# A recommendation kernel on Trainium2: the attention's weighing and sum moved to VectorE with tokens on partitions

## The chip, the cores and the metric

The kernel runs on one core of one Trainium2 chip. The metric is the device time of one execution in microseconds (us). The engines of the core are TensorE (PE in the profile; PEld is its weight load), VectorE (DVE), ScalarE (ACT), GpSimd (POOL) and SyncE (SP). SBUF is the working memory with 128 partitions; PSUM takes TensorE's products and can be read and written by VectorE and ScalarE.

## The reference

For 4096 users, each with a history of 200 items, the kernel computes a small attention over the history and then a three-layer head. All numbers are float32; an embedding has D = 64 elements.

```
u = u_emb[user]; it = i_emb[item]; c = c_emb[cate]; h = i_emb[hist]      # h: 200 x 4096 x 64
feat = concat([h, it, h - it, h * it])                                   # 256 wide
a = dice(feat @ au_W1 + au_b1, au_alpha, axis=1)                         # 36 wide, moments over the users
w = a @ au_W2 + au_b2                                                    # one weight per user and history line
cur = sum over the 200 lines of w * h
z = concat([u, it, c, cur])
z = dice(z @ W1 + b1, ...); z = dice(z @ W2 + b2, ...); out = z @ W3 + b3
dice(x, alpha) = x * (p + alpha * (1 - p)),  p = sigmoid((x - mean) / sqrt(var + 1e-8))
```

The moments of the attention's dice are taken over all 4096 users of one history line, so a line's gate can only be computed when all tiles of that line have passed the first layer.

## The kernel before, in words

A history line is cut into eight tiles of 512 users (ND = 8). One *step* k handles one tile; there are 200 x 8 = 1600 steps. Line and column of a step are `l, c = divmod(k, ND)`.

**Gathers.** `fetch(k)` issues the tile's rows: 16 indirect DMAs of 128 rows each on GpSimd's queue (line L119 of the profile), into `rows[k % 4]`, with tokens (users) on partitions and 16 x 64 elements along them. Each takes its 128 row numbers from one column of `idx`, which SyncE loads a line ahead. In every second line one of the 16 is left to SyncE: for column c = 7 (`SIDES`) SyncE reads 128 addresses into registers and issues 128 single-row DMAs into `side` (`rows_by_sync`, spread over the steps by `ask`); ScalarE copies that side into `rows` (L301). So a step has 16 gathers, or 15 in one of 16 steps.

**First layer.** `turn(k-1)`: four VectorE transposes (L150) turn the rows, in blocks of 32 x 32, into `hT`, with the features on partitions and two users' groups side by side; TensorE multiplies `hT` by `blk_h` into the PSUM tile `px`; ScalarE copies `hT` to the PSUM tile `ph` (L304). `product(k-1)`: VectorE multiplies `ph` by the item's features `itT` into `hm` (L307), and TensorE adds `hm` times `blk_m` to `px`. `hidden(k-2)`, one step later: VectorE adds the item's own part `itp` to `px`, giving x in `xs` (L292), and `measure` takes its statistics (L297). After the eighth tile `moments` turns the statistics into a scale and a shift (small operations, L313 to L327, and L164 to L166).

**Second layer,** nine steps behind the gather (`LAG = 9`): `gate` has ScalarE compute the dice's gate into the PSUM tile `pg` (L280, L281), `weights` multiplies it by x into `y` in SBUF (L284), and TensorE multiplies `y` by `blk_w`, blocks of ones, into `wb`: the sum over the 36 hidden values appears as w on all the partitions of a user's group. `weigh` then has VectorE compute (wb + b2) * hT in place (L288) and add it to `curT[c]` (L289).

**Order.** Everything is issued in the order of the program (a manual schedule); each engine works through its own list, with semaphores between engines. The order within a step is that of `step`:

```python
fetch(k); hidden(k - 2); measure(k - 2); moments after the eighth tile; gate(k - 9)
turn(k - 1); weights(k - 9); product(k - 1); weigh(k - 9)
```

The 200 lines are run as a hardware loop of three passes of 54 lines (`LPB = 54`) and 38 lines written out behind it; at each pass's end all engines meet at a barrier. Ahead of the loop stand the item's gathers (8 tiles, with transposes and `itp`) and the loading of the weights. In the written-out tail the last steps are interleaved with the head's gathers of categories and users (16 tiles); then follow the head's layers, with moments over all users between them.

Buffers: `rows` 4, `hT` 9 (kept until `weigh`), `xs` 8, `curT` 8, each 128 x 1024 float32.

Of the kernel before, what the change touches and what calls it, by code (L numbers as in the profile page):

```python
# [9 lines left out]
I32 = mybir.dt.int32  # L10
# [10 lines left out]
LPB = 54  # L21
ROWS = 4
LAG = 9
XR = 8
IDX = 3
SIDES = (7,)
EVERY = 2
PART = 8
# [5 lines left out]
def din_kernel(  # L34
# [67 lines left out]
    hT = [make(f"hT{i}", P, CD) for i in range(LAG)]  # L102
    xs = [make(f"xs{i}", P, CD) for i in range(XR)]
    itT = [make(f"itT{c}", P, CD) for c in range(ND)]
    curT = [make(f"curT{c}", P, CD) for c in range(ND)]
    hm = make("hm", P, CD)
    y = make("y", P, CD)
# [23 lines left out]
    def load_hist_ids(i, l, whole):  # L131
# [3 lines left out]
        if whole:  # L135
            nc.sync.dma_start(idx[i][:, NC:], r_hist[ds(l, 1), NC * P :].rearrange("l p -> p l"))

    def load_addresses(m, l):
        nc.sync.dma_start(addr[m % 3], r_hist[ds(l, 1), NC * P :])

    def scale_addresses(m):
        nc.vector.tensor_scalar_mul(addr[m % 3], addr[m % 3], ROW)
# [27 lines left out]
    blk_i = make("blk_i", P, P)  # L170
    blk_m = make("blk_m", P, P)
    blk_w = make("blk_w", P, P)
    au_w = make("au_w", P, 4, A)
# [7 lines left out]
    def attention_weights():  # L181
        nc.vector.memset(eps, EPS)
        for t in (blk_h, blk_i, blk_m, blk_w, au_bias, au_al, au_w2):
            nc.vector.memset(t, 0.0)
        nc.sync.dma_start(au_bias2, au_b2.partition_broadcast(P))
        for e in range(2):
            w = au_W1.rearrange("(g d) a -> d g a", d=D)[e * S : (e + 1) * S]
            for g in range(2):
                r = quarter(e, g)
                nc.sync.dma_start(au_w[r], w)  # L190
                for q, (a0, n) in enumerate(halves):
                    c, a = quarter(q, g, n), slice(a0, a0 + n)
                    nc.vector.tensor_add(blk_h[r, c], au_w[r, 0, a], au_w[r, 2, a])
                    nc.vector.tensor_sub(blk_i[r, c], au_w[r, 1, a], au_w[r, 2, a])
                    nc.vector.tensor_copy(blk_m[r, c], au_w[r, 3, a])
                    nc.vector.memset(blk_w[r, quarter(q, g)], 1.0)
# [25 lines left out]
    lanes, lane = (y[:, ts(i, P)].bitcast(I32) for i in range(2))  # L222
# [34 lines left out]
    def rows_by_sync(m, part):  # L257
        p0 = part * PART
        _, at = nc.values_load_multi_w_load_instructions(
            addr[m % 3][:, p0 : p0 + PART],  # L260
            engines=(mybir.EngineType.SP,), min_val=0, max_val=ROW * (V - 1),
            skip_runtime_bounds_check_because="the DMA checks the address against the table",
        )
        for j, a in enumerate(at):
            row = flat[ds(a, ROW)].rearrange("(o d) -> o d", o=1)
            nc.sync.dma_start(side[m % 3].bitcast(U8)[p0 + j : p0 + j + 1], row)

    def has_side(k):
        l, c = divmod(k, ND)
        return c in SIDES and l % EVERY == EVERY - 1  # L270
# [12 lines left out]
    def weights(k):  # L283
        nc.vector.tensor_mul(y, pg, xs[k % XR])  # L284
        layer(wb, [(blk_w, y)])

    def weigh(k):
        nc.vector.scalar_tensor_tensor(wb, wb, au_bias2, hT[k % LAG], ALU.add, ALU.mult)  # L288
        nc.vector.tensor_add(curT[k % ND], wb, curT[k % ND])  # L289

    def hidden(k):
        nc.vector.tensor_add(xs[k % XR], px, itp[k % ND])  # L292
# [6 lines left out]
    def turn(k):  # L299
        if has_side(k):  # L300
            nc.scalar.copy(rows[k % ROWS][:, TD - 1], side[k // ND // EVERY % 3])  # L301
        transpose(hT[k % LAG], rows[k % ROWS])
        layer(px, [(blk_h, hT[k % LAG])], last=False)
        nc.scalar.copy(ph, hT[k % LAG])  # L304

    def product(k):
        nc.vector.tensor_mul(hm, ph, itT[k % ND])  # L307
        layer(px, [(blk_m, hm)], first=False)
# [44 lines left out]
    def ask(k, end):  # L353
        m, part = divmod(k + 1, EVERY * ND)
        if m * EVERY + EVERY - 1 < end:
            rows_by_sync(m, part)

    def steps(l0, n, more):
        for k in range(n * ND):
            l, c = divmod(k, ND)  # L360
            far = l + EVERY
            if c == 0 and l + 1 < n + more:
                load_hist_ids((l + 1) % IDX, l0 + l + 1, l % EVERY == EVERY - 1)
            if l % EVERY == EVERY - 1 and far < n + more * EVERY:
                if c == 2:
                    load_addresses(far // EVERY, l0 + far)
                if c == 4:
                    scale_addresses(far // EVERY)
            ask(k, n + more * EVERY)
            step(k)  # L370

    with tc.manual_schedule():
        load_ids(ids[0], r_item)
        load_hist_ids(0, 0, True)
        load_addresses(0, EVERY - 1)
# [6 lines left out]
        for t in curT:  # L382
            nc.vector.memset(t, 0.0)
# [6 lines left out]
        scale_addresses(0)  # L390

        for c in range(ND + 1):
            if c < ND:
                for n in range(TD):
                    j = column(c, n)
                    gather(rows[c % ROWS], ids[0][:, j : j + 1], n, i_emb)
            if c:
                transpose(itT[c - 1], rows[(c - 1) % ROWS])
                layer(px, [(blk_i, itT[c - 1])])
                nc.scalar.activation(itp[c - 1], px, AF.Identity, bias=au_bias)  # L400
        layer(px, [(blk_m, hm)])
        nc.vector.memset(rows[-1 % ROWS], 0.0)
        ask(-1, L)
        head_weights()

# [6 lines left out]
    za = [hT[(K - LAG + c) % LAG] for c in range(ND)]  # L412
    zb = [xs[(K - XR + j) % XR] for j in range(2)]
# [6 lines left out]
    def head_fetch(k, j):  # L420
        c, u = divmod(j, 2)
        for n in range(TD):
            i = column(c, n)
            gather(rows[k % ROWS], ids[1 + u][:, i : i + 1], n, (c_emb, u_emb)[u])

    def head_layer(j):
        c, u = divmod(j, 2)
        if u == 0:
            pairs = ((2, ucT[j % 4]), (1, itT[c]), (3, curT[c]))
        else:  # L430
            pairs = ((0, ucT[j % 4]),)
        layer(px, [(w1a[:, f], t) for f, t in pairs], first=not u, last=u == 1)
        layer(ph[:S], [(w1b[:, f], t) for f, t in pairs], first=not u, last=u == 1)
        if u:
            nc.scalar.activation(za[c], px, AF.Identity, bias=b1a)
            measure_head(0, c, za[c])
            nc.scalar.activation(zb[c // 4][ts(c % 4, S)], ph[:S], AF.Identity, bias=b1b)
            if c % 4 == 3:
                measure_head(1, c // 4, zb[c // 4])

    with tc.manual_schedule():
        steps(BODY, L - BODY, 0)
        for j in range(2 * ND + 2):
            if j < 2 * ND:
                head_fetch(K + j, j)
            step(K + j, last=K - 1)
            if 1 <= j <= 2 * ND:
                transpose(ucT[(j - 1) % 4], rows[(K + j - 1) % ROWS])
# [3 lines left out]
        def head_moments(i, same):  # L452
            mv = small.tile([P, 2], F32, tag=f"hmv{i}", name="hmv")
            nc.vector.bn_aggr(mv, zst[i].rearrange("p c s -> p (c s)"))
            pm = (pg, wb)[i % 2]
# [12 lines left out]
        temps = [y, hm, ucT[2], ucT[3]]  # L468
# [8 lines left out]
        pz = [px, ph, pg, wb]  # L477
# [5 lines left out]
        for c in range(ND + 1):  # L483
            if c < ND:
                dice(curT[c], za[c], na, al1a, ala)
                q = ts(c % 4, S)
                for h in range(2):
                    cols = ts(h, CH)
                    nc.tensor.matmul(pz[c % 4][:, cols], w2a, curT[c][:, cols], start=True, stop=False)  # L489
# [6 lines left out]
        for c in range(ND):  # L496
            g, q = divmod(c, 4)
            dice(curT[c], z2[c], n2, al12, al2)
            layer(pz[2 * g], [(w3[:, q], curT[c])], first=q == 0, last=q == 3)
# [53 lines left out]
```

## Time and profile before

| what | value |
|---|---|
| time of 3 runs | median 32463.89 us (32462.97 to 32466.95) |
| profiled execution, its own time | 32463.26 us |
| its span, first to last instruction | 32461.4 us |
| mean granted TensorE clock | 0.672 |
| busy: POOL, DVE, PE, ACT | 75%, 52%, 39%, 19% |
| DMA packets of GpSimd's queue | 828288 packets, 849.82 MB |
| DMA packets of SyncE's queue | 75024 packets, 17.07 MB |
| gather, issue to landing, median | 2.4 us |

The profile cuts the span into 40 slices, and over the whole of it these look alike: the 1600 steps fill it almost entirely.

```profile
PE   3333333333333333333333333333333333333334
DVE  4555555555555555555555555555555555555554
POOL 7777777777777777777777777777777777777776
```

(Each digit is the busy share of a slice in tenths.)

How to read the lines: a group row names the line, the engine, the operation, out<-in by the program's names, the shapes and the count; behind the bar stand the busy time in us, the mean of one in ns, then the idle time of that engine just before these instructions and what ended most of it. "issue" means that the engine waited for nothing that the profile shows. A timeline row has the start in us, the duration in us, the engine, the line, the operation and the idle time before it in brackets. [...]

### The profile page before, as it was taken

To read this page: it belongs to the slowest core of one execution; us is meant where nothing else is said; L and a number is where in the kernel's file an instruction comes from. 1 tells how busy PE (TensorE), PEld (TensorE's weight loads), DVE (VectorE), ACT (ScalarE), POOL (GpSimd) and SP (SyncE) were. 2 spreads that over 40 slices of the span, in tenths; PEclk is the share of its full clock that TensorE was granted. 3 is DMA by queue.
4 is the path that set the end of the run, shared out by engine and by line. 5 is a ranking of instruction groups with operands and counts; after the bars stand their busy time and mean duration, and the time that the engine had idled before them with its cause. 6 is when DMAs were issued, how large, how long until landed. Compare 5 with 4: busy or idle time off the path is not lost. (4 is left out here: it accounts for less than half of the span.)

```text
span 32461.4 us, 129600 instructions
## 1 busy us (share of the span) xinstructions
PE 12533.5 (39%) x19644; PEld 4905.3 (15%) x19644; DVE 16887.4 (52%) x20453; ACT 6125.0 (19%) x5585; POOL 24422.7 (75%) x25889
## 2 busy tenths in 40 slices
PE   3333333333333333333333333333333333333334
PEld 1111111111111111111111111111111111111111
DVE  4555555555555555555555555555555555555554
ACT  1111111111111111111111111111111111111111
POOL 7777777777777777777777777777777777777776
PEclk6666666666666666666666666666666666666666
DMA  1111111111111111111111111111111111111111
GB/s 28 27 27 27 27 27 27 27 27 27 27 27 27 27 27 27 27 27 27 27 27 27 27 27 27 27 27 27 27 27 27 27 27 27 27 27 27 27 27 22
DMA packets 904331, 875.35 MB, mean 27 GB/s; under 512 B 489212, under 2 KB 489312, under 8 KB 903456
## 3 DMA queue, kind: packets, MB, share of 16 engines
q0 software_dynamic: 828288, 849.82, 11.8%
q1 hardware_dynamic: 75024, 17.07, 0.3%
q14 instruction: 718, 5.88, 0.1%
q8 instruction: 157, 2.57, 0.0%
q10 hardware_dynamic: 144, 0.00, 0.0%
HBM read 865.03 MB, written 0.13 MB: 27 GB/s over the span
## 5 line engine op out<-in xcount | busy, mean ns | idle before, releaser
L119 POOL DMA_INDIRECT rows<-in_L_rec_i_emb,idx x25500 | 24059.8, 944 | 7788.7 <-issue 7340.6
L155 PE MATMUL px<-hT,blk_h 128*128 128x512 f32 x6404 | 5975.9, 1089 | 19595.4 <-DVE hT L150 19579.4
L150 DVE STREAM_TRANSPOSE hT<-rows 64x512 f32<-64x512 f32 x6404 | 4519.0, 706 | 11321.0 <-DMA rows<-in_L_rec_i_emb,idx 10920.7
L304 ACT COPY ph<-hT 128x1024 f32<-128x1024 f32 x1601 | 1628.1, 1017 | 23432.5 <-DVE hT L150 23432.5
L155 PEld LDWEIGHTS px<-hT,blk_h 128*128 128x128 f32 x6404 | 1802.1, 312 | 22654.0 <-DVE hT L150 22456.1
L288 DVE SCALAR_TENSOR_TENSOR wb<-wb,au_bias,hT 128x1024 f32<-128x1024 f32 x1609 | 2079.8, 1293 | 3527.2 <-PE wb L155 3527.2
L155 PE MATMUL wb<-y,blk_w 128*128 128x512 f32 x6436 | 3873.2, 733 | 67.7 <-DVE y L284 67.7
L155 PE MATMUL px<-hm,blk_m 128*128 128x512 f32 x6408 | 3012.8, 592 | 1.2 <-ACT itp L400 1.2
L155 PEld LDWEIGHTS wb<-y,blk_w 128*128 128x128 f32 x6436 | 1805.0, 281 | 2878.3 <-issue 1978.5
L297 DVE BATCH_NORM_STATS2 st<-xs 128x6 f32<-128x512 f32 x3204 | 2060.4, 685 | 55.4
L280 ACT ACTIVATE pg<-xs,sh,rs 128x1024 f32<-128x1024 f32 x1609 | 1943.8, 1208 | 367.6 <-DVE y L284 365.0
L289 DVE TENSOR_TENSOR curT<-wb,curT 128x1024 f32<-128x1024 f32 x1609 | 1969.8, 1224 | 54.8
L284 DVE TENSOR_TENSOR y<-pg,xs 128x1024 f32<-128x1024 f32 x1609 | 1969.5, 1224 | 54.3 <-ACT pg L281 3.7
L292 DVE TENSOR_TENSOR xs<-px,itp 128x1024 f32<-128x1024 f32 x1602 | 1941.4, 1212 | 27.4 <-PEq L407 26.9
L307 DVE TENSOR_TENSOR hm<-ph,itT 128x1024 f32<-128x1024 f32 x1601 | 1943.5, 1214 | 0.0
L281 ACT ACTIVATE pg<-pg,au_al,au_1al 128x1024 f32<-128x1024 f32 x1609 | 1893.8, 1177 | 54.1
L155 PEld LDWEIGHTS px<-hm,blk_m 128*128 128x128 f32 x6408 | 1220.1, 190 | 1586.4 <-issue 1583.6
L164 ACT ACTIVATE std<-var,eps 128x1 f32<-128x1 f32 x201 | 59.1, 294 | 1931.2 <-DVE var L327 1931.2
L280 ACT ACT_TABLE_LOAD x205 | 263.0, 1283 | 57.4 <-PEq L407 38.7
L164 ACT ACT_TABLE_LOAD x203 | 260.4, 1283 | 7.5 <-PE pg L462 4.0
L317 DVE COPY other<-mv 32x2 f32<-32x2 f32 x804 | 154.4, 192 | 15.1
L119 POOL DMA_INDIRECT rows<-in_L_rec_i_emb,ids x128 | 120.9, 945 | 40.6 <-issue 37.2
(149 smaller groups left out, 1221.1 us busy)
## 6 DMA issues: line engine op xcount, KB each, us to landing
rows<-in_L_rec_i_emb,idx POOLq DMA_INDIRECT x25500, 2.4
side<-in_L_rec_i_emb SPq DMA_DIRECT2D x12800, 0.2 KB
idx<-in_r_hist SPq DMA_DIRECT2D x200, 63.5 KB
rows<-in_L_rec_i_emb,ids POOLq DMA_INDIRECT x128, 2.4
rows<-in_L_rec_c_emb,ids POOLq DMA_INDIRECT x128, 2.3
rows<-in_L_rec_u_emb,ids POOLq DMA_INDIRECT x128, 2.4
idx<-in_r_hist SPq DMA_DIRECT2D x100, 0.5 KB
addr<-in_r_hist SPq DMA_DIRECT2D x100, 0.5 KB
```

The source lines that it names most:

```text
L119: nc.gpsimd.indirect_dma_start(out=dst[:, n, :], out_offset=None, in_=table, in_offset=bass.IndirectOffsetOnAxis(ap=ids, axis=0),)
L150: nc.vector.transpose(by_tile(dst[ts(e, D)], i), of[ts(i, D), :, ts(e, S)])
L155: nc.tensor.matmul(dst[:, ts(i, CH)], lhsT, rhs[:, ts(i, CH)], start=(first and j == 0), stop=(last and j == len(pairs) - 1), skip_group_c ...
L280: nc.scalar.activation(pg, xs[k % XR], AF.Sigmoid, bias=shifts[i], scale=rstds[i])
L281: nc.scalar.activation(pg, pg, AF.Identity, bias=au_al, scale=au_1al)
L284: nc.vector.tensor_mul(y, pg, xs[k % XR])
L288: nc.vector.scalar_tensor_tensor(wb, wb, au_bias2, hT[k % LAG], ALU.add, ALU.mult)
L289: nc.vector.tensor_add(curT[k % ND], wb, curT[k % ND])
L292: nc.vector.tensor_add(xs[k % XR], px, itp[k % ND])
L297: nc.vector.bn_stats(stats[l % 3][:, 2 * c + i, :], xs[k % XR][:, ts(i, CH)])
L304: nc.scalar.copy(ph, hT[k % LAG])
L307: nc.vector.tensor_mul(hm, ph, itT[k % ND])
```

## The change

The second layer is computed with tokens on partitions.

- `weights` now multiplies gate and x into the PSUM tile `py`; VectorE transposes `py` into `pg` in 32 x 32 blocks, which puts tokens on partitions and hidden values along them; `reduce_sum` over 32 values gives `sums`; four small operations add the two halves of a user's hidden values and the bias into `w`, one value per token.
- `weigh` multiplies the *untransposed* rows by `w`, broadcast over the 64 elements, into `py`, and adds `py` to `cur[c]`. So the rows must live until then: `ROWS` goes from 4 to 12; `hT` shrinks to two buffers. The head transposes `cur` before it uses it (`head_layer`).
- TensorE's product with `blk_w` and the tiles `wb`, `ph` and `y` go; so does ScalarE's copy of `hT`. `product` reads `hT` itself.
- `px` becomes two PSUM buffers, `hidden` and `measure` take x at k - 3 instead of k - 2, and `LAG` goes from 9 to 10. `product(k-1)` now stands right behind `turn(k-1)`, ahead of `weights`.
- The loop has 36 lines instead of 54 (five passes and 20 lines behind it). The tile that SyncE helps with is column 5 instead of 7 of every second line; its requests are spread by a small class `Queue` over 16 steps, beginning two steps ahead of the pair of lines.
- The item's gathers use two of the row buffers; some weights made before the loop lie in row buffers that are cleared afterwards; the head borrows row buffers for its temporaries.

```diff
-LPB = 54
-ROWS = 4
-LAG = 9
+LPB = 36
+ROWS = 12
+LAG = 10
...
-SIDES = (7,)
-EVERY = 2
-PART = 8
+SIDES = (5,)
+PERIOD = 2
+BY_SP = ((1, 5),)
...
-    px = psum.tile([P, CD], F32, name="px")
-    ph = psum.tile([P, CD], F32, name="ph")
+    px = [psum.tile([P, CD], F32, name=f"px{i}") for i in range(2)]
     pg = psum.tile([P, CD], F32, name="pg")
-    wb = psum.tile([P, CD], F32, name="wb")
+    py = psum.tile([P, CD], F32, name="py")
...
     def weights(k):
-        nc.vector.tensor_mul(y, pg, xs[k % XR])
-        layer(wb, [(blk_w, y)])
+        nc.vector.tensor_mul(py, pg, xs[k % XR])
+        nc.vector.transpose(pg, py)
+        nc.vector.reduce_sum(sums, pg.rearrange("p (n a) -> p n a", a=S), axis=mybir.AxisListType.X)
+        for i in range(2):
+            for g in range(2):
+                nc.vector.scalar_tensor_tensor(
+                    w[quarter(i, g)],
+                    sums[quarter(0, g), ts(i, TD)], au_bias2[quarter(0, g)], sums[quarter(1, g), ts(i, TD)],
+                    ALU.add, ALU.add,
+                )

     def weigh(k):
-        nc.vector.scalar_tensor_tensor(wb, wb, au_bias2, hT[k % LAG], ALU.add, ALU.mult)
-        nc.vector.tensor_add(curT[k % ND], wb, curT[k % ND])
+        part = py.rearrange("p (n d) -> p n d", d=D)
+        nc.vector.tensor_mul(part, rows[k % ROWS], w.unsqueeze(2).to_broadcast([P, TD, D]))
+        nc.vector.tensor_add(cur[k % ND], py, cur[k % ND])

     def hidden(k):
-        nc.vector.tensor_add(xs[k % XR], px, itp[k % ND])
+        nc.vector.tensor_add(xs[k % XR], px[k % 2], itp[k % ND])
...
-        transpose(hT[k % LAG], rows[k % ROWS])
-        layer(px, [(blk_h, hT[k % LAG])], last=False)
-        nc.scalar.copy(ph, hT[k % LAG])
+        transpose(hT[k % TURNED], rows[k % ROWS])
+        layer(px[k % 2], [(blk_h, hT[k % TURNED])], last=False)

     def product(k):
-        nc.vector.tensor_mul(hm, ph, itT[k % ND])
-        layer(px, [(blk_m, hm)], first=False)
+        nc.vector.tensor_mul(hm, hT[k % TURNED], itT[k % ND])
+        layer(px[k % 2], [(blk_m, hm)], first=False)
...
         if has(k):
             fetch(k)
-        if has(k - 2):
-            hidden(k - 2)
-            measure(k - 2)
-            if (k - 2) % ND == ND - 1:
-                moments((k - 2) // ND)
+        if has(k - 3):
+            hidden(k - 3)
+            measure(k - 3)
+            if (k - 3) % ND == ND - 1:
+                moments((k - 3) // ND)
         if has(k - LAG):
             gate(k - LAG)
         if has(k - 1):
             turn(k - 1)
+            product(k - 1)
         if has(k - LAG):
             weights(k - LAG)
-        if has(k - 1):
-            product(k - 1)
-        if has(k - LAG):
             weigh(k - LAG)
...
+        def when(self, q):
+            m, i = divmod(q, self.per)
+            return m * PERIOD * ND // len(self.tiles) + i * self.span // self.per - self.lead
...
+    queues = (SyncQueue(mybir.EngineType.SP, BY_SP, 8, 2, PERIOD * ND // len(BY_SP), side, addr),)
...
-            pairs = ((2, ucT[j % 4]), (1, itT[c]), (3, curT[c]))
+            pairs = ((2, ucT[j % 4]), (1, itT[c]))
         else:
-            pairs = ((0, ucT[j % 4]),)
+            transpose(hT[c % TURNED], cur[c].rearrange("p (n d) -> p n d", d=D))
+            pairs = ((3, hT[c % TURNED]), (0, ucT[j % 4]))
```

More of the change, by code (lines that the diff above doesn't have):

```diff
@@ L134, in load_hist_ids @@
         )
[L135 to L142, printed above, removed]
+        for s, c in enumerate(SIDES):
+            if c not in by_address:
+                j = NC + s
+                nc.sync.dma_start(
+                    idx[i][:, j : j + 1], r_hist[ds(l, 1), j * P : (j + 1) * P].rearrange("l p -> p l")
+                )
     def by_tile(t, i):
@@ L221, in din_kernel @@
     same_b = make("same_b", P, P)
-    lanes, lane = (y[:, ts(i, P)].bitcast(I32) for i in range(2))
+    lanes, lane = (rows[-2].rearrange("p n d -> p (n d)")[:, (5 + i) * P : (6 + i) * P].bitcast(I32) for i in range(2))
     def head_weights():
@@ L268, in has_side, with start, take, by_address @@
+    class SyncQueue(Queue):
+        def start(self, m, dst, row):
+            nc.sync.dma_start(dst, row)
+        def take(self, m):
+            return self.buffers[m % self.n]
+    queues = (SyncQueue(mybir.EngineType.SP, BY_SP, 8, 2, PERIOD * ND // len(BY_SP), side, addr),)
+    def by_address(l):
+        return {c for q in queues for t, c in q.tiles if t == l % PERIOD}
     def has_side(k):
         l, c = divmod(k, ND)
-        return c in SIDES and l % EVERY == EVERY - 1
+        return c in by_address(l)
@@ L345, in step, with ask @@
             turn(k - 1)
+            product(k - 1)
         if has(k - LAG):
             weights(k - LAG)
-        if has(k - 1):
-            product(k - 1)
-        if has(k - LAG):
             weigh(k - LAG)
[L353 to L356, printed above, removed]
+    def ask(k, l0, n, more):
+        for q in queues:
+            for what, m in q.events(k, n * len(q.tiles) // PERIOD + (more and 2)):
+                what(m, l0)
     def steps(l0, n, more):
@@ L381, in din_kernel @@
             nc.vector.memset(t, 0.0)
-        for t in curT:
+        for t in cur:
             nc.vector.memset(t, 0.0)
@@ L395, in din_kernel @@
                     j = column(c, n)
-                    gather(rows[c % ROWS], ids[0][:, j : j + 1], n, i_emb)
+                    gather(rows[c % 2], ids[0][:, j : j + 1], n, i_emb)
             if c:
[L398 to L403, printed above, removed]
+                transpose(itT[c - 1], rows[(c - 1) % 2])
+                layer(px[c % 2], [(blk_i, itT[c - 1])])
+                nc.scalar.activation(itp[c - 1], px[c % 2], AF.Identity, bias=au_bias)
+        for t in px:
+            layer(t, [(blk_m, hm)])
+        for k in range(-16, 0):
+            ask(k, 0, L, 0)
         head_weights()
+        for t in rows[2:]:
+            nc.vector.memset(t, 0.0)
     if BODY:
@@ L423, in head_fetch @@
             i = column(c, n)
-            gather(rows[k % ROWS], ids[1 + u][:, i : i + 1], n, (c_emb, u_emb)[u])
+            gather(spare[j % 3], ids[1 + u][:, i : i + 1], n, (c_emb, u_emb)[u])
     def head_layer(j):
@@ L484, in din_kernel @@
             if c < ND:
[L485 removed]
+                dice(cur[c], za[c], na, al1a, ala)
                 q = ts(c % 4, S)
@@ L497, in din_kernel @@
             g, q = divmod(c, 4)
-            dice(curT[c], z2[c], n2, al12, al2)
-            layer(pz[2 * g], [(w3[:, q], curT[c])], first=q == 0, last=q == 3)
+            dice(cur[c], z2[c], n2, al12, al2)
+            layer(pz[2 * g], [(w3[:, q], cur[c])], first=q == 0, last=q == 3)
             if q < 3:
```

114 lines of the change are left out of this document (70 added, 44 removed).

## The prediction

> **What bounds the kernel now.** I read the page first: the engines' busy shares, then the costliest groups.
>
> ```profile
> span 32461.4 us, 129600 instructions
> PE 12533.5 (39%) x19644; PEld 4905.3 (15%) x19644; DVE 16887.4 (52%) x20453; ACT 6125.0 (19%) x5585; POOL 24422.7 (75%) x25889
> L119 POOL DMA_INDIRECT rows<-in_L_rec_i_emb,idx x25500 | 24059.8, 944 | 7788.7 <-issue 7340.6
> ```
>
> POOL does almost nothing but gathers. The 25500 of the history take 24059.8 us busy and 7788.7 us before them, together 31848.5 us, or 1249.0 ns for one; 16 make a step of 19.98 us. The idle part is put down to "issue": POOL waits for nothing. The view of waits says the same and shows who waits for POOL.
>
> ```profile
> DVE hT L150 <- DMA rows<-in_L_rec_i_emb,idx: 10920.7, 1547, 8.8
> POOL rows L119 <- issue: 7450.9, 24392, 10.2
> DVE wb L288 <- PE wb L155: 3527.2, 1609, 3.9
> ```
>
> VectorE stands 10920.7 us, 6.8 us a step, before the transposes until rows land. So the bound is the sequence of gathers on POOL, and everything else has slack. One step in the timeline:
>
> ```profile
> 10017.13 0.95 POOL L119 DMA_INDIRECT rows<-in_L_rec_i_emb,idx  x1 [0.30 <-issue]
> 10017.31 2.88 DVE L150 STREAM_TRANSPOSE hT<-rows 64x512 f32<-64x512 f32 x4 [7.05 <-DMA rows<-in_L_rec_i_emb,idx]
> ...
> 10020.23 1.23 DVE L284 TENSOR_TENSOR y<-pg,xs 128x1024 f32<-128x1024 f32 x1
> ...
> 10021.37 1.22 DVE L307 TENSOR_TENSOR hm<-ph,itT 128x1024 f32<-128x1024 f32 x1
> ```
>
> What lies outside the gathers: a loop boundary (two of them, and the loop's exit, in the timeline) and the end after the last gather.
>
> ```profile
> 8756.23 0.94 POOL L119 DMA_INDIRECT rows<-in_L_rec_i_emb,idx  x1 [0.31 <-issue]
> 8761.27 0.94 POOL L119 DMA_INDIRECT rows<-in_L_rec_i_emb,idx  x1 [4.09 <-issue]
> 17354.80 0.94 POOL L119 DMA_INDIRECT rows<-in_L_rec_i_emb,idx  x1 [0.30 <-issue]
> 17365.96 0.94 POOL L119 DMA_INDIRECT rows<-in_L_rec_i_emb,idx  x1 [10.21 <-issue]
> 25963.11 0.94 POOL L119 DMA_INDIRECT rows<-in_L_rec_i_emb,idx  x1 [3.00 <-issue]
> 32329.66 0.94 POOL L119 DMA_INDIRECT rows<-in_L_rec_u_emb,ids  x1 [0.30 <-issue]
> ```
>
> A boundary costs 3.8 us (4.09 less the usual 0.30) or 9.9 us, the exit 2.7 us; the end is 32461.4 - 32330.6 = 131 us.
>
> **The change, part by part.**
>
> *Gathers.* The side tile moves from column 7 to 5 of every second history line; still one tile in two lines has 15 gathers, so 25500 stay, and SyncE still fetches 100 sides of 128 rows. At an unchanged 1249 ns this part is 0. SyncE's address loads and the scaling on VectorE keep their counts, some ten steps ahead of their use: 0.
>
> *Removed.* The wb products and the ACT copy to ph go, and with them VectorE's wait for wb (3527.2 us, 2.2 us a step). All of it lay beside POOL's gathers: gain 0. What is late next is what was late before, the landing of rows.
>
> *Added on VectorE*, per step: a PSUM transpose, a sum over 32, four small sums. The multiply by w takes the place of the L288 operation. Nearest rows by shape:
>
> ```profile
> L502 DVE STREAM_TRANSPOSE xs<-px 128x1024 f32<-128x1024 f32 x1 | 1.2, 1249 | 3.4 <-PE px L155 3.4
> L289 DVE TENSOR_TENSOR curT<-wb,curT 128x1024 f32<-128x1024 f32 x1609 | 1969.8, 1224 | 54.8
> L317 DVE COPY other<-mv 32x2 f32<-32x2 f32 x804 | 154.4, 192 | 15.1
> ```
>
> 1.25 for the transpose; 1.22 for the sum, which reads as many elements as L289 (at least half of that, at most twice); 4 x 0.19 = 0.8 for the small ones. VectorE goes from 16887.4/1600 = 10.6 to about 13.8 us of a 19.98 us step. Hidden under the gathers; without that cover it would be 3.2 us a step, 5200 us in all.
>
> *New wait.* A row buffer is now free only after weigh, ten steps after its gathers began. With 12 buffers the gather of step k needs the weigh of step k-2, and VectorE ends that about 14 us after rows k-3 landed, 20 us or more ahead of the gather. Queued behind this wait on POOL would be every later gather; I cost it at 0, and by 1 us for every us that VectorE falls more than 20 us behind.
>
> *x a step later, two px buffers.* L292 hardly waited before; the extra step of lag ends under the head's gathers. 0.
>
> *Loop of 36 instead of 54 lines.* Five passes instead of three: two more boundaries, 3.8 to 9.9 us each, 8 to 20 us; I take 14. The end: the last tile's sum needs a transpose (2.88 us) and its share of the head's product after the last gather: 5 us, between 0 and 10.
>
> *Operand places.* This is the step that decides. L307 read ph from PSUM; now `hm` reads hT and itT, both in SBUF. The multiply of weigh reads rows and w, both in SBUF. Before, no long VectorE operation beside a gather had two SBUF inputs, so no row has the price. What rows have is this: POOL and VectorE do stop one another.
>
> ```profile
> L142 DVE TENSOR_SCALAR addr<-addr x100: 203/205/466, 43.5 to 31605.0; 1x128 int32<-1x128 int32 x100
> L317 DVE COPY other<-mv x804: 156/161/419, 208.2 to 32027.3; 32x2 f32<-32x2 f32 x161
> L319 DVE TENSOR_TENSOR total<-mv,other x201: 160/161/163, 209.1 to 32027.5; 128x2 f32<-128x2 f32 x101
> L119 POOL DMA_INDIRECT rows<-in_L_rec_i_emb,idx x25500: 940/944/969, 162.9 to 32010.1; - x200
> ```
>
> (minimum, median, maximum in ns.) The longest of all 25500 gathers, 969 ns, is this one:
>
> ```profile
> 14722.07 0.20 DVE L142 TENSOR_SCALAR addr<-addr 1x128 int32<-1x128 int32 x1
> 14722.12 0.97 POOL L119 DMA_INDIRECT rows<-in_L_rec_i_emb,idx  x1 [0.30 <-issue]
> ```
>
> It starts 0.05 us into an L142 and loses 25 ns: a gather needs something at its start that VectorE then holds. And an operation with two SBUF inputs, in the same shape twice:
>
> ```profile
> 8.68 0.18 DVE L193 TENSOR_TENSOR blk_h<-au_w 32x32 f32<-32x32 f32 x1
> ...
> 9.33 0.24 DVE L193 TENSOR_TENSOR blk_h<-au_w 32x32 f32<-32x32 f32 x1
> 9.35 0.94 POOL L119 DMA_INDIRECT rows<-in_L_rec_i_emb,ids  x1 [0.30 <-issue]
> ```
>
> The one that meets a gather's start loses 0.06 us. So the start of a gather and a two-input operation exclude each other; whoever has begun, goes on. If that holds for 1024 elements too, a gather that starts under one waits for its end, and POOL has no slack to take it up. Length of the hold: from 32 elements (0.18) to 1024 (1.22) it grows by 1.05 ns an element, so 1.08 us. I let it begin 0.06 us after the operation's start, an estimate: the L142 above had begun 0.05 us before the gather that it held up. Bounds per operation: 0 (no gather waits) and 1.08 (it starts just with the hold).
>
> Now the phase. The transposes start 0.18 us after a gather's start (10017.31 against 10017.13). hm takes the place of y in the order, 2.92 us after the first transpose T: it holds from T+2.98 to T+4.06. Gathers start at T-0.18+1.25n, the third at T+3.57: it waits 0.49. In other steps
>
> ```profile
> 8740.01 0.94 POOL L119 DMA_INDIRECT rows<-in_L_rec_i_emb,idx  x1 [0.30 <-issue]
> 8740.28 2.88 DVE L150 STREAM_TRANSPOSE hT<-rows 64x512 f32<-64x512 f32 x4 [6.91 <-DMA rows<-in_L_rec_i_emb,idx]
> ...
> 8782.49 2.88 DVE L150 STREAM_TRANSPOSE hT<-rows 64x512 f32<-64x512 f32 x4 [1.90 <-DMA rows<-in_L_rec_i_emb,idx]
> 8782.49 0.94 POOL L119 DMA_INDIRECT rows<-in_L_rec_i_emb,idx  x1 [0.30 <-issue]
> ```
>
> the offset is 0.27 and 0.00, the wait 0.58 and 0.31. I take 0.4. From then on gathers run in step with hm: T+4.06, 5.31, 6.56, 7.81, 9.06. Between hm's start and weigh's multiply lie hm to py 1.14 (as y to hm above), py 1.22, transpose 1.25, sum 1.22, small sums 0.8, and 0.03 before each that depends on its neighbour: 5.75. The multiply starts at T+8.67, holds to T+9.81, and the gather of T+9.06 waits 0.75. Were the sequence 0.3 shorter it would be 0.45; 0.35 longer, and that gather would slip in ahead and wait 0. I take 0.7. (With phases at random each wait would be 1.08 x 1.08/(2 x 1.25) = 0.47 on average.) Together 1.1 us a step, 1760 us in 1600 steps.
>
> [...]
>
> **Sum**, against the profiled execution's own 32463.3 us (span 32461.4; the median is 32463.9, the same within 1 us): 32463 + 1760 + 14 + 5 = 32463 + 1779, about 34240 us, 5.5% slower.
>
> **Rivals.**
>
> *No gather waits, not slower.* The 25 ns of L142 come from a copy-like integer operation, not from one with two float inputs, and L319, with two SBUF inputs, never took over 163 ns although 201 of them ran beside gathers. If the gather takes its index before, or between two elements of VectorE's read, the price is 0 and the time is 32463 + 19 = 32482 us, no change. Decisive point: whether a gather's maximum exceeds 969 ns by much. Against it: L193's 0.06 us, and L319 holds for two elements only. A true gain would need a gather under 1249 ns; nothing in the change touches that.
>
> *One collision of two.* The multiply comes later than T+9.0, or the sum is short, and one operation escapes: 0.1 to 0.8 us a step, 32640 to 33760 us; at 0.4, 33120.
>
> *Full holds.* The gather starts just behind both operations' starts, or the broadcast multiply takes two cycles an element: 1.4 to 2.16 us a step, 34720 to 35940 us.
>
> *Another wait takes over.* VectorE, at 13.8 of 21 us, would have to lose 7 us a step; PE loses 6436 of its products and ACT its copy. Little speaks for it.
>
> **How the numbers follow.** About 0.2%, 65 us, is what a measurement of this kernel can tell from no change. Both collide at 0.8 to 1.4 us a step (33760 to 34720): 0.60. One escapes: 0.15. Full holds: 0.08. No wait, within 0.2%: 0.12. Another wait, slower: 0.03. Faster: 0.02. So slower 0.86, same 0.12, faster 0.02. The range 32900 to 35000 holds the first case, most of the second and half of the third.
>
> **What would show it.** Right: gathers of two kinds in the changed profile, most at 944 ns, two in each step near 1.3 and 1.7 us, always under hm and under weigh's multiply; the mean of L119 near 1013 ns (944 + 1100/16), idle before it still 0.30; transposes still waiting for rows. Wrong: all gathers at 944 ns (first rival); long gathers under one operation only (second); gathers waiting for VectorE before their start, or VectorE without idle time (last). The step of the phases is wrong if the waits are of other sizes than 0.4 and 0.7.

## The result and the profile after

| | before | after |
|---|---|---|
| time, median (4 runs each, same chip) | 32464.1 us (32462.97 to 32466.95) | 34913.3 us (34910.9 to 34917.6) |
| ratio after to before | | 1.0754, interval 1.0736 to 1.0773 |
| span of the profiled execution | 32461.4 us | 34911.1 us |
| mean granted TensorE clock | 0.672 | 0.621 |

The changed kernel is 7.5% slower; 34240 us had been predicted, with 32900 to 35000 as the range. The page of the changed kernel:

```profile
span 34911.1 us, 126622 instructions
PE 9750.6 (28%) x13212; PEld 3590.8 (10%) x13212; DVE 22289.1 (64%) x30144; ACT 4500.3 (13%) x3987; POOL 26841.2 (77%) x25889
L120 POOL DMA_INDIRECT rows<-in_L_rec_i_emb,idx x25500 | 26471.9, 1038 | 7812.9 <-issue 7481.1
L367 DVE TENSOR_TENSOR hm<-hT,itT 128x1024 f32<-128x1024 f32 x1601 | 1961.2, 1225 | 178.0 <-DVE hT L149 14.4
L333 DVE STREAM_TRANSPOSE pg<-py 128x1024 f32<-128x1024 f32 x1610 | 2037.4, 1265 | 55.3
L345 DVE TENSOR_TENSOR py<-rows,w 128x1024 f32<-128x1024 f32 x1610 | 1984.9, 1233 | 55.7
L334 DVE TENSOR_REDUCE sums<-pg 128x32 f32<-128x1024 f32 x1610 | 1972.1, 1225 | 54.7
L337 DVE SCALAR_TENSOR_TENSOR w<-sums,au_bias 32x16 f32<-32x16 f32 x6440 | 1458.6, 226 | 212.4
```

The engine that lost busy time (PE, from 12533.5 to 9750.6 us) brought nothing, and the one that gained most (DVE, from 16887.4 to 22289.1) is not the one that cost. POOL issues the same 25500 gathers, now under L120, and they are busy 26471.9 us instead of 24059.8: 2412.1 of the 2449.7 us by which the span grew. The idle time before them went up by 24 us only. The waiting is *inside* the gathers' recorded duration, so a view of waits can't show it. That view of the changed kernel (who waits <- for whom: us, times, longest):

```profile
DVE hT L149 <- DMA rows<-in_L_rec_i_emb,idx: 11197.0, 1579, 8.3
...
POOL rows L120 <- DVE py L345: 19.1, 1, 19.1
```

VectorE still stands 11197.0 us, 7.0 us a step, until rows land, so it has not become the bound. A single wait of POOL for VectorE is new; it is taken up below. All gathers of the history in the changed kernel, durations in ns as minimum, median and maximum:

```profile
L120 POOL DMA_INDIRECT rows<-in_L_rec_i_emb,idx x25500: 940/944/1975, 162.9 to 34446.4; - x200
```

The median is where it was; the maximum has doubled. Two gathers in each step are long. One step in the timeline of the changed kernel:

```profile
10011.85 0.94 POOL L120 DMA_INDIRECT rows<-in_L_rec_i_emb,idx  x1 [0.30 <-issue]
10012.10 2.88 DVE L149 STREAM_TRANSPOSE hT<-rows 64x512 f32<-64x512 f32 x4 [7.63 <-DMA rows<-in_L_rec_i_emb,idx]
...
10015.09 1.23 DVE L367 TENSOR_TENSOR hm<-hT,itT 128x1024 f32<-128x1024 f32 x1
10015.60 1.53 POOL L120 DMA_INDIRECT rows<-in_L_rec_i_emb,idx  x1 [0.30 <-issue]
10016.23 1.23 DVE L332 TENSOR_TENSOR py<-pg,xs 128x1024 f32<-128x1024 f32 x1
...
10017.43 0.94 POOL L120 DMA_INDIRECT rows<-in_L_rec_i_emb,idx  x1 [0.30 <-issue]
10017.49 1.26 DVE L333 STREAM_TRANSPOSE pg<-py 128x1024 f32<-128x1024 f32 x1
...
10018.79 1.23 DVE L334 TENSOR_REDUCE sums<-pg 128x32 f32<-128x1024 f32 x1
...
10020.05 1.00 DVE L337 SCALAR_TENSOR_TENSOR w<-sums,au_bias 32x16 f32<-32x16 f32 x4
...
10021.08 1.23 DVE L345 TENSOR_TENSOR py<-rows,w 128x1024 f32<-128x1024 f32 x1
10021.18 1.95 POOL L120 DMA_INDIRECT rows<-in_L_rec_i_emb,idx  x1 [0.30 <-issue]
```

The gather of 10015.60 starts under `hm` and takes 1.53 us, 0.59 more than the usual 0.94. It ends 0.81 us after hm does (10017.13 against 10016.32). The gather of 10021.18 starts 0.10 us into the multiply by w, takes 1.95 us, and again ends 0.82 us after it. The gathers under L332, L333 and L334 take 0.94 us, but in this step they start in the last 0.1 us of these operations, where a hold would be over, so they don't show what such an operation does. The kernel before does: 1607 of its gathers start under y (L284, one input in SBUF), 0.14 to 1.06 us behind its start, and none takes over 0.954 us. Summed over the trace by the operation under which the gather starts, 1592 gathers under hm lost 506 ns on average (806 us), and 1609 under the multiply 1002 ns (1612 us, the few in the head's gathers included).

### The profile page after: what moved, and what is told of

Same layout as the page of the kernel before. It is cut to its first block, busy times and chain, and to the rows that moved or that the text cites. A ratio compares the mean times of both kernels' runs of the same rounds, so it can differ in the third digit from the quotient of the medians.

```text
span 34911.1 us, 126622 instructions
## 1 busy us (share of the span) xinstructions
PE 9750.6 (28%) x13212; PEld 3590.8 (10%) x13212; DVE 22289.1 (64%) x30144; ACT 4500.3 (13%) x3987; POOL 26841.2 (77%) x25889
## 3 DMA queue, kind: packets, MB, share of 16 engines
q0 software_dynamic: 828288, 849.82, 13.9%
## 5 line engine op out<-in xcount | busy, mean ns | idle before, releaser
L120 POOL DMA_INDIRECT rows<-in_L_rec_i_emb,idx x25500 | 26471.9, 1038 | 7812.9 <-issue 7481.1
L149 DVE STREAM_TRANSPOSE hT<-rows 64x512 f32<-64x512 f32 x6404 | 4520.2, 706 | 11369.0 <-DMA rows<-in_L_rec_i_emb,idx 11197.0
L154 PE MATMUL px<-hm,blk_m 128*128 128x512 f32 x6412 | 3846.5, 731 | 1.2 <-ACT itp L450 1.2
L367 DVE TENSOR_TENSOR hm<-hT,itT 128x1024 f32<-128x1024 f32 x1601 | 1961.2, 1225 | 178.0 <-DVE hT L149 14.4
L333 DVE STREAM_TRANSPOSE pg<-py 128x1024 f32<-128x1024 f32 x1610 | 2037.4, 1265 | 55.3
L345 DVE TENSOR_TENSOR py<-rows,w 128x1024 f32<-128x1024 f32 x1610 | 1984.9, 1233 | 55.7
L154 PEld LDWEIGHTS px<-hm,blk_m 128*128 128x128 f32 x6412 | 1714.8, 267 | 2879.5 <-issue 1930.1
L334 DVE TENSOR_REDUCE sums<-pg 128x32 f32<-128x1024 f32 x1610 | 1972.1, 1225 | 54.7
L346 DVE TENSOR_TENSOR cur<-py,cur 128x1024 f32<-128x1024 f32 x1610 | 1970.2, 1224 | 55.8
L332 DVE TENSOR_TENSOR py<-pg,xs 128x1024 f32<-128x1024 f32 x1610 | 1971.9, 1225 | 17.2 <-ACT pg L329 17.1
L337 DVE SCALAR_TENSOR_TENSOR w<-sums,au_bias 32x16 f32<-32x16 f32 x6440 | 1458.6, 226 | 212.4
L120 POOL DMA_INDIRECT rows<-in_L_rec_c_emb,ids x128 | 126.2, 986 | 39.0 <-issue 36.0
L120 POOL DMA_INDIRECT rows<-in_L_rec_i_emb,ids x128 | 120.9, 945 | 40.7 <-issue 36.9
```

The lines of the kernel that those rows point to most:

```text
L120: nc.gpsimd.indirect_dma_start(out=dst[:, n, :], out_offset=None, in_=table, in_offset=bass.IndirectOffsetOnAxis(ap=ids, axis=0),)
L149: nc.vector.transpose(by_tile(dst[ts(e, D)], i), of[ts(i, D), :, ts(e, S)])
L154: nc.tensor.matmul(dst[:, ts(i, CH)], lhsT, rhs[:, ts(i, CH)], start=(first and j == 0), stop=(last and j == len(pairs) - 1), skip_group_c ...
L332: nc.vector.tensor_mul(py, pg, xs[k % XR])
L333: nc.vector.transpose(pg, py)
L334: nc.vector.reduce_sum(sums, pg.rearrange("p (n a) -> p n a", a=S), axis=mybir.AxisListType.X)
```

## The experiments

The **theory**: a gather that starts while VectorE runs an operation with two inputs in SBUF waits until that operation has almost ended; where such operations stand against the gathers' beat sets the price. The **rivals**: each new VectorE operation costs POOL a fixed time whatever its operands are; or something else of the change costs (the longer VectorE list, the row buffers kept longer, the shorter loop), and the long gathers only show where it is paid. The kernels below that are quoted without a number of runs were run once. Beside them, on the same chip, the kernel before gave 32464.32 us (one run), or 32465.2 us (median of 15 runs) where `LAG = 9` or the memset is tried.

**One input of the multiply to PSUM.** The weights w are put into a part of `py`, and the product goes to `pg`. VectorE has the same operations.

```diff
-    w = make("w", P, TD)
+    w = py[:, :TD]
...
-        part = py.rearrange("p (n d) -> p n d", d=D)
+        part = pg.rearrange("p (n d) -> p n d", d=D)
...
-        nc.vector.tensor_add(cur[k % ND], py, cur[k % ND])
+        nc.vector.tensor_add(cur[k % ND], pg, cur[k % ND])
```

> The changed kernel, but w lies in PSUM (in the tile py, dead at that time) and the product of weigh goes to pg, so that weigh's multiply has one SBUF input instead of two; same work. Theory (a gather that starts under a VectorE operation with two SBUF inputs waits for its end): the 1612 us of waits under weigh's multiply go, the 806 us under hm stay, about 33300 us. Rival (the added VectorE work slows POOL, whatever its operands): unchanged, about 34910 us. Rival (only hm's operands matter, the waits under the multiply come from its broadcast): unchanged, or up to 200 us either way.

Measured: 33177.9 us, 1735 less than the changed kernel. The timeline of this kernel, at its hm and at its multiply:

```profile
10008.08 1.23 DVE L367 TENSOR_TENSOR hm<-hT,itT 128x1024 f32<-128x1024 f32 x1
10008.75 1.37 POOL L120 DMA_INDIRECT rows<-in_L_rec_i_emb,idx  x1 [0.30 <-issue]
...
10014.14 1.23 DVE L345 TENSOR_TENSOR pg<-rows,py 128x1024 f32<-128x1024 f32 x1
10014.17 0.94 POOL L120 DMA_INDIRECT rows<-in_L_rec_i_emb,idx  x1 [0.30 <-issue]
```

The multiply has its old length, a gather starts 0.03 us into it, and it takes 0.94 us. Only hm holds gathers now, 680 us in all instead of 806. A fixed price per operation is out: the operation is still there and costs nothing. But the edit did two things at once. The four small sums, now written to PSUM, take 240 ns each instead of 226, so the multiply starts 6.06 us behind hm instead of 5.99, and 1597 of the 1609 gathers under it start 0.02 to 0.05 us behind its start, at an edge where gathers pass under operations with two SBUF inputs too (last section). So this run alone can't tell the operand's place from the phase. Only ten gathers start well inside the multiply, 0.09 to 0.95 us behind its start; none of them takes over 0.95 us. The kernel with both edits, below, parts the two causes.

**hm's input back in PSUM.** `hm` reads `ph`, ScalarE's copy of hT, as before the change; `px` is one buffer again, x is taken at k - 2, and the product stands behind the weights. `LAG` stays 10 here, so that `xs` with its eight buffers holds x of a later tile when the second layer reads it: this kernel weighs with another tile's x. The operations and their sizes are those of a full kernel.

```diff
-    px = [psum.tile([P, CD], F32, name=f"px{i}") for i in range(2)]
+    px = [psum.tile([P, CD], F32, name="px0")] * 2
+    ph = psum.tile([P, CD], F32, name="ph")
...
+        nc.scalar.copy(ph, hT[k % TURNED])
...
-        nc.vector.tensor_mul(hm, hT[k % TURNED], itT[k % ND])
+        nc.vector.tensor_mul(hm, ph, itT[k % ND])
...
-        if has(k - 3):
-            hidden(k - 3)
+        if has(k - 2):
+            hidden(k - 2)
...
-            product(k - 1)
         if has(k - LAG):
             weights(k - LAG)
+        if has(k - 1):
+            product(k - 1)
...
```

> The changed kernel, but product takes hT from PSUM again: one px buffer, ScalarE's copy to ph, x at k-2, product behind weights, all as before; weigh's multiply keeps its two SBUF inputs, but starts about 8.8 to 9.0 us after the first transpose instead of 8.9 to 9.0 behind a collision. Theory: no waits under hm; under the multiply the wait follows the phase, 0.1 to 0.25 us a step: 32660 to 32900 us. Rival (each such operation has a price of its own, 1.0 us for the multiply): 34911 - 806 = 34105 us.

Measured: 32703.7 us; only the multiply holds gathers, some 1100 of them for 209 us in all. The same with `LAG = 9`, where x is the right tile's:

> As e2_ph, but with a lag of 9 instead of 10, as x at k-2 asks for with eight xs buffers. Theory: the same work at the same phases, so 32680 to 32730 us, waits under weigh's multiply alone. Rival (fixed price of the multiply): 34105 us.

Measured: 32689.1 us. A row of the page of this kernel, with `LAG = 9`:

```profile
L121 POOL DMA_INDIRECT rows<-in_L_rec_i_emb,idx x25500 | 24271.0, 952 | 7794.1 <-issue 7405.5
```

And its timeline at a multiply:

```profile
10018.75 1.22 DVE L346 TENSOR_TENSOR py<-rows,w 128x1024 f32<-128x1024 f32 x1
10019.31 1.47 POOL L121 DMA_INDIRECT rows<-in_L_rec_i_emb,idx  x1 [0.30 <-issue]
```

The hold is there, but the multiply now holds some 1100 gathers for 0.19 us each instead of 1609 for 1.00. So the two prices do not add: freeing hm took 2201 of the 2412 us off the gathers, freeing the multiply (with the later start named above) 1731, together far more than there was. In the changed kernel hm's wait shifts the gathers so that one comes just behind the multiply's start (0.08 to 0.10 us in 1569 of 1609 cases). Held alone, the multiply's gathers cost 211 us and hm's 680; the pair, at a fixed distance, costs 2412.

**Both inputs in PSUM,** the two edits together (`LAG = 9`):

> The changed kernel with both long operations at one SBUF input: w in PSUM as in e1_w_psum, and ph, one px buffer, x at k-2, lag 9 as in e2b_ph. All of the new second layer's VectorE work remains. Theory: no gather waits; left over are the start (18 us), the loop boundaries (6 us) and the end (7 us): 32490 to 32510 us, 0.1% above the kernel before. Rival (VectorE's added 3 us a step cost POOL something in themselves): over 32600 us.

Measured: 32475.3 us (10 runs, 32474.1 to 32477.8) beside 32465.2 us (15 runs), ratio 1.0003, interval 0.9994 to 1.0013. It is 15 us below the expectation, since the wait at the start (below) is not there with `LAG = 9`. From the page of this kernel:

```profile
PE 12186.8 (38%) x13212; PEld 3749.8 (12%) x13212; DVE 22683.2 (70%) x30132; ACT 6125.6 (19%) x5586; POOL 24422.2 (75%) x25889
L121 POOL DMA_INDIRECT rows<-in_L_rec_i_emb,idx x25500 | 24059.3, 944 | 7794.0 <-issue 7310.5
```

The durations of its gathers:

```profile
L121 POOL DMA_INDIRECT rows<-in_L_rec_i_emb,idx x25500: 938/944/962, 162.8 to 32014.8; - x200
```

And its timeline at hm and at the multiply:

```profile
283.26 1.23 DVE L369 TENSOR_TENSOR hm<-ph,itT 128x1024 f32<-128x1024 f32 x1
283.85 0.95 POOL L121 DMA_INDIRECT rows<-in_L_rec_i_emb,idx  x1 [0.30 <-issue]
284.51 1.23 DVE L346 TENSOR_TENSOR pg<-rows,py 128x1024 f32<-128x1024 f32 x1
285.10 0.94 POOL L121 DMA_INDIRECT rows<-in_L_rec_i_emb,idx  x1 [0.30 <-issue]
```

No gather is long, and this time not by its phase: 1581 gathers start 0.07 to 1.0 us behind hm's start and 1587 behind the multiply's, and none takes over 0.962 us. The kernel with `LAG = 9` above differs from this one only in the place of w and of the product, and there a gather 0.56 us behind the multiply's start takes 1.47 us where here one at 0.59 us takes 0.94. That is the operand's place. VectorE is busier than in the changed kernel (22683.2 us against 22289.1), the second layer still runs on VectorE with tokens on partitions, the 12 row buffers and the loop of 36 lines are still there, and all of that together costs 10 us. The two px buffers and the changed order of a step are not in this kernel; they are in the one with w in PSUM, which is 714 us above the kernel before: 680 us under hm and 34 us for all else. The second rival is out too.

**The hm edit alone, in the kernel before:** ph goes and hm reads hT; nothing else of the change.

```diff
-        nc.scalar.copy(ph, hT[k % LAG])
...
-        nc.vector.tensor_mul(hm, ph, itT[k % ND])
+        nc.vector.tensor_mul(hm, hT[k % LAG], itT[k % ND])
```

> The kernel before, with one edit: hm reads hT in SBUF and ScalarE's copy to ph is left out; everything else as before. Theory: hm starts 4.06 us after the first transpose, so a gather that starts under it waits 0.24 to 0.32 us a step: 32850 to 32980 us, and gathers over 970 ns appear under hm alone. Rival (the price belongs to the new second layer): 32464 us. Rival (fixed price 0.50 us as in the changed kernel): 33270 us.

Measured: 32882.6 us, 418 more than before. Timeline of this kernel:

```profile
10011.86 1.22 DVE L306 TENSOR_TENSOR hm<-hT,itT 128x1024 f32<-128x1024 f32 x1
10012.50 1.40 POOL L119 DMA_INDIRECT rows<-in_L_rec_i_emb,idx  x1 [0.31 <-issue]
```

1498 gathers under hm lost 237 ns each, 355 us; the wait comes with this one operand. The rest is not a hold: all gathers of this kernel are 3 ns longer in the median (947 instead of 944), also those of the item, which run ahead of the first hm. In the mean of those that hm doesn't hold it is 2.4 ns (945.9 instead of 943.5), and 25500 x 2.4 ns is 61 us.

**Short operations.** If a gather waits for the running operation's end, four quarters in place of one operation should shorten the wait.

```diff
-        nc.vector.tensor_mul(part, rows[k % ROWS], w.unsqueeze(2).to_broadcast([P, TD, D]))
+        for i in range(4):
+            q = ts(i, TD // 4)
+            nc.vector.tensor_mul(part[:, q], rows[k % ROWS][:, q], w[:, q].unsqueeze(2).to_broadcast([P, TD // 4, D]))
...
-        nc.vector.tensor_mul(hm, hT[k % TURNED], itT[k % ND])
+        for i in range(4):
+            q = ts(i, CD // 4)
+            nc.vector.tensor_mul(hm[:, q], hT[k % TURNED][:, q], itT[k % ND][:, q])
```

> The changed kernel, with hm and weigh's multiply each issued in four pieces of a quarter of the columns; same data, six more VectorE instructions a step. Theory (the hold lasts as long as one instruction): a gather waits at most for a piece, under 0.3 us; about 0.13 us a step in all, up to 0.27: 32700 to 32930 us. Rival (back-to-back pieces keep POOL out together): 34900 us or more.

Measured: 33021.0 us, some 90 us above the expectation. The gathers of this kernel:

```profile
L120 POOL DMA_INDIRECT rows<-in_L_rec_i_emb,idx x25500: 942/947/1221, 163.1 to 32558.9; - x200
```

The longest wait is now 1221 - 947 = 274 ns, less than a quarter takes (0.42 us): the hold is that of the single instruction and not of the row of them. Under the pieces of the multiply 1620 gathers lost 183 ns (296 us), under those of hm some 1200 lost 141 ns (169 us): 0.29 us a step, where 0.13 and at most 0.27 had been expected. The rest of the miss is the 3 ns on every gather (2.4 in the mean, again some 60 us) that the kernel with the one edit showed as well; here too the item's gathers have them. What in a build gives these 3 ns stays open.

**The phase.** 0.27 us of other work (a memset) ahead of the multiply puts its start behind that of the gather that waited longest.

```diff
+    pad = make("pad", P, 256)
...
+        nc.vector.memset(pad, 0.0)
         nc.vector.tensor_mul(part, rows[k % ROWS], w.unsqueeze(2).to_broadcast([P, TD, D]))
```

> The changed kernel with more work: a memset of 128x256 on VectorE ahead of weigh's multiply, which then starts 0.2 to 0.3 us later. Theory: the gather that now starts 0.1 us behind the multiply's start will start ahead of it and not wait; the 1612 us go although VectorE does more: 33200 to 33400 us. Rival (a fixed price for each such operation, or a load effect): 34911 us or more.

Measured: 33406.4 us, 6 us above the expectation and 1507 below the changed kernel. Timeline of this kernel:

```profile
10020.42 0.27 DVE L346 MEMSET pad<- 128x256 f32 x1
10020.43 0.95 POOL L121 DMA_INDIRECT rows<-in_L_rec_i_emb,idx  x1 [0.30 <-issue]
10020.73 1.24 DVE L347 TENSOR_TENSOR py<-rows,w 128x1024 f32<-128x1024 f32 x1
10021.68 1.09 POOL L121 DMA_INDIRECT rows<-in_L_rec_i_emb,idx  x1 [0.30 <-issue]
```

More work for VectorE made the kernel 4.3% faster. The gather that used to wait a microsecond starts under the memset and slips through; the next comes 0.95 us behind the multiply's start and waits 0.15 us. So the multiply's waits did not go, as expected, but fell from 1612 to 230 us; hm's fell from 806 to 683, for the gathers now reach hm a little later in it. Both operations read the same operands as in the changed kernel, so this difference is the phase's.

**A version that beats both.** Where each of the two operations has one input in PSUM, the gathers are back at 1.249 us each, and still the bound, so each gather less is worth that much. So more sides were left to SyncE: first one tile in every line instead of every second (100 gathers fewer), then two tiles in every line (300 fewer), each with the both-in-PSUM kernel as its base.

```diff
-BY_SP = ((1, 5),)
+BY_SP = ((0, 5), (1, 5))
```

> As e3b_both, and SyncE fetches the side tile of every line instead of every second: 100 gathers fewer on POOL, 12800 more single-row DMAs on SyncE. Theory (POOL's gathers are the bound): 100 x 1.249 = 125 us less than e3b_both, 32365 to 32385 us, below the kernel before by 0.3%. Rival (SyncE's rows come late, or slow the gathers' landing): above e3b_both.

Measured: 32353.0 us (6 runs), ratio to before 0.9966, interval 0.9953 to 0.9978; 122 us less than its base, against 100 x 1.249 = 125.

```diff
-SIDES = (5,)
+SIDES = (2, 5)
...
-BY_SP = ((1, 5),)
+BY_SP = ((0, 2), (0, 5), (1, 2), (1, 5))
...
-            for what, m in q.events(k, n * len(q.tiles) // PERIOD + (more and 2)):
+            for what, m in q.events(k, n * len(q.tiles) // PERIOD + (more and 3)):
```

> As e7b_sp1, with SyncE fetching two tiles of every line (columns 2 and 5): 300 gathers fewer than in e3b_both, 51200 single-row DMAs in all. Theory (gathers on POOL are the bound, 1.249 us each): 375 us less than e3b_both's 32475, 32090 to 32120 us, 1.1% below the kernel before. Rival (SyncE, at 128 x 0.43 us a tile 110 us of each line's 157 us, comes late, or VectorE, at 14 of 19.5 us a step, becomes the bound): above 32200 us.

Measured: 32143.7 us (4 runs), ratio 0.9901, interval 0.9883 to 0.9919: 1.0% below the kernel before. It is 332 us less than its base, not 300 x 1.249 = 375. What is missing stands in its gaps: the loop's boundaries cost more (8.8 to 10.6 us each, with 4.6 to 6.4 in its base), and waits came at the start, the longest in its timeline:

```profile
201.53 0.95 POOL L121 DMA_INDIRECT rows<-in_L_rec_i_emb,idx  x1 [0.30 <-issue]
219.54 0.94 POOL L121 DMA_INDIRECT rows<-in_L_rec_i_emb,idx  x1 [17.06 <-DVE rows L461]
```

## Why the prediction was right, and where its sizes were off

**The bound** held: POOL's gathers set the time in every kernel here, with VectorE 52% busy in the kernel before, 64% in the changed one and 70% in the both-in-PSUM kernel. **The mechanism** held: two long gathers in each step, under hm and under the multiply, at an unchanged idle time of 0.30 us before them. The hold's length was also nearly right. It was put from 0.06 to 1.14 us behind an operation's start; by the timeline of the changed kernel a held gather's usual 0.94 us begin 1.10 us behind it. That the two inputs in SBUF matter is shown by the kernel without them: with one of the two moved to PSUM in both operations, no gather takes over 0.962 us, where 1.975 had been the most. What it is that a gather's start needs, no run here shows. One of the rows on which the prediction built the hold does not belong to it: L142 has one input in SBUF (addr), so the theory of these experiments does not explain the 25 ns of the gather under it.

The sum was 1779 us, the measured difference 2449, and its terms compare so:

| term | predicted | measured |
|---|---|---|
| gathers under the multiply | 0.7 us a step, 1120 us | 1.00 us, 1612 us |
| gathers under hm | 0.4 us a step, 640 us | 0.50 us, 806 us |
| boundaries and exit of the loop | 14 us | 5.7 us |
| end | 5 us | 6.9 us |
| row buffers at the start | 0 | 18.8 us |

*The multiply's wait* was mis-sized through the small sums. The distance from hm's start to the multiply's was put at 5.75 us and is 10021.08 - 10015.09 = 5.99 us. Of the 0.24 us, 0.20 is the four small sums: 226 ns each, 1.00 us in a row, where the nearest row, a copy of 32x2, had given 0.8. In the prediction's own terms a distance longer by 0.24 makes the wait 0.75 + 0.24 = 0.99 us, and 1.00 was measured. The point at which the gather would slip in ahead, 0.35 longer, was missed by 0.1 us; the kernel with the memset crosses it. Up to that point each 0.1 us of distance is 160 us of the kernel's time, and beyond it most of the multiply's 1612 us are gone. That the sequence ended on the near side of it is luck: the margin was 0.1 us, and the small sums alone had been put 0.20 us too short.

*hm's wait* was taken as 0.4 us from offsets of 0.18, 0.27 and 0.00 between gather and transposes. In the changed kernel the median offset is 0.16 us, which by the same working gives 0.16 + 0.31 = 0.47, near the measured 0.50; the choice had leaned too low.

*Row buffers at the start*, costed at 0, are the one wrong step. In the steady state no gather waits for weigh, as forecast. Once it does. The timeline of the changed kernel:

```profile
201.64 0.94 POOL L120 DMA_INDIRECT rows<-in_L_rec_i_emb,idx  x1 [0.30 <-issue]
...
208.06 0.91 DVE L457 MEMSET rows<- 128x1024 f32 x1 [0.16 <-issue]
...
220.18 1.23 DVE L345 TENSOR_TENSOR py<-rows,w 128x1024 f32<-128x1024 f32 x1
221.69 0.94 POOL L120 DMA_INDIRECT rows<-in_L_rec_i_emb,idx  x1 [19.10 <-DVE py L345]
```

At the start VectorE is behind by the ten clearings of row buffers (L457, the last at 208.06), and the gather into the third buffer waits for the first weigh: 19.10 less 0.30 us. The working looked at a step in the middle only. With `LAG = 9`, a step of slack more, the both-in-PSUM kernel has no such wait.

*Boundaries:* five gaps where there were three, but smaller ones. Together they take 22.1 us above the usual idle time, before 16.4. The first one in the timeline of the changed kernel:

```profile
6348.58 0.94 POOL L120 DMA_INDIRECT rows<-in_L_rec_i_emb,idx  x1 [6.36 <-issue]
```

*VectorE's load* was put at 13.8 us a step and is 22289.1/1600 = 13.9; it is hidden, as forecast. The removed products brought nothing, as forecast. By its time the measurement lies not in the main case (0.8 to 1.4 us a step, 33760 to 34720 us, a chance of 0.60) but in the range of the rival "Full holds" (1.4 to 2.16, 34720 to 35940 us, a chance of 0.08): the waits are 1.51 us a step. The stated range of 32900 to 35000 us holds it because it took in a part of that rival. By its mechanism the rival is half true: the multiply's gather starts almost with the hold, hm's does not, and the broadcast multiply takes 1233 ns, about as long as hm (1225). "No gather waits" and "One collision of two" are excluded by the long gathers under both.

## What to carry to other kernels

Where GpSimd's gathers are the bound, as here, look at each long VectorE operation for two inputs in SBUF: in these kernels one operand in PSUM left the operation about as long as it was (hm 1214 ns with ph in the kernel before and 1225 with hT in the changed one, the multiply 1.23 us in the timelines with either) and took the gathers' waits away, 7% of the time. The operand has to get there: for hm it is a copy on ScalarE of 1.02 us a step, hidden here, and the small sums take 240 ns instead of 226 when they write to PSUM. Such waits stood inside the gather's own duration (a mean of 1038 ns instead of 944, a maximum of 1975 instead of 969), so look for them there and not among the waits. Price them by phase and not on average: the multiply, at a fixed distance, cost 1.00 us in every step and with 0.27 us of other work ahead of it 0.14, and hm's wait shifted the beat into the multiply's (680 and 211 us alone, 2412 together).

## What the runs showed of the hardware that was not expected

- In the changed kernel a held gather ends 0.81 us (0.80 to 0.83) after the VectorE operation's end, whichever operation held it and however long it had waited; an unhindered one takes 0.94 us. Only a gather's start is held: there the 22300 gathers of the history that start under neither of the two operations take 943.5 ns in the mean, the same as in the kernel before, although hm starts while a gather is under way in 1548 of 1601 cases; hm is no longer for it (1225 ns in the mean).
- The hold begins sharply. In the kernel with the memset the seven gathers that start 0.01 to 0.04 us behind hm's start take 0.94 us, the one at 0.06 us takes 1.98, and from there the time falls by what the start is later, to 0.94 at 1.10. (With ph and `LAG = 10`, two at 0.04 us behind the multiply's start already take 1.99, so the edge is sharp to a few hundredths of a microsecond, no better.) In the changed kernel 1569 of the 1609 gathers under the multiply start 0.08 to 0.10 us behind its start, just inside the edge, and take 1.93 to 1.97 us.
- The granted TensorE clock does not go with the time: 0.672 in the kernel before, 0.621 after and 0.588 in the both-in-PSUM kernel, which takes 0.03% longer than before.
- A transpose of 128x1024 from PSUM to PSUM takes 1265 ns, about as much as a multiply of that size (1225 ns), and a sum of 32x16 with two inputs 226 ns.
